# The last 64 tokens of an image as a whole chunk of 128 on TensorE, with new step costs for the planner

## The chip, the core and the metric

The kernel runs on one NeuronCore of a Trainium2 chip. The metric is the device time of one execution in microseconds (us), lower is better. The kernel before was run three times: 1931.54, 1933.95 and 1940.33 us; the median is 1933.95 us.

## What is computed

The input x is 16 images of 56 x 56 positions with 128 channels, float32 throughout. The reference has three parts in a row, each added to its input:

```
x = x + window_attention(group_norm(x))      # 7x7 windows, shifted by 3, 4 heads of 32
t = x as tokens: 16 images of 3136 tokens of 128
t = t + linear_attention(layer_norm(t))      # q, k = elu(.)+1; running sums of k*v over time
t = t + recurrent(layer_norm(t))             # Wx with batch norm; y_t = sigmoid(wx_t + y_{t-1} V^T)
```

Linear attention is computed in chunks: inside a chunk a product of q and k, masked to be causal, and between chunks a running state of 128 x 129 (the sum of k times v, and of k). 3136 tokens are 24 chunks of 128 and one chunk of 64.

## The kernel before, in words

**Stages.** The first stage, up to about 1729 us of the profiled span, treats the images one after the other, overlapped. The second, some 200 us long, is the recurrent scan with its output. The change is in the first stage alone.

**Work of one image in the first stage.** The tokens of an image lie in an SBUF buffer `xt` with 128 tokens on the partitions, in 25 columns of 128 channels, and are handled in seven groups (`GROUPS`, L238): six of four chunks of 128 tokens, and a last one of one chunk of 64 tokens, here called the short group. `chunks_of` (L277) gives a group's part of `xt`; for the short group that is 64 partitions.

- `turned` (L576): each group is transposed on TensorE (`transpose_group`, L558, instruction line L562); ScalarE copies the result to the image buffer `xw` (L604, L606), VectorE takes its statistics (L614). A small chain follows for group normalisation: VectorE L657 to L679, TensorE L661 and L675, GpSimd `again` (L652, L653) and a power (L683), ScalarE L687, TensorE L692.
- `window_row` (L733), eight times an image, one row of eight windows each: VectorE gathers the windows (`gather_windows`, L747), TensorE projects (L757, L784), scores (L808, 64 matmul instructions on weight tiles of 32 x 49), GpSimd subtracts the maximum and scales (L834, L853), TensorE transposes (L863) and mixes (L882, 64 instructions on tiles of 49 x 32), ScalarE writes the result to `oT_buf` (`mix_out`, L917).
- `token_group` (L1031), seven times an image: GpSimd adds the output bias (L1044), TensorE projects (`project`, L1054), VectorE adds (L1063). `layer_scale` (L948) then takes statistics (L958), makes a scale on GpSimd (`join`, L965 to L972), scales (L978) and transposes (L562). TensorE makes q and k (L1095, twice), v (`values`, L1142), transposes k (L1165, not in the short group), the products of k and q (`products`, L1180), the outputs (`attend`, L1209 and L1212) and the state (`gather`, L1220, not in the short group). A second `layer_scale` and a product (L1309) prepare the recurrent part; ScalarE stages it (L1329), and SyncE's DMA queue stores it (L1351) and the tokens (L1015).

One float32 matmul is two instructions in the trace; a transpose is one. The weight tile of an instruction is given as rows*columns. In the short group L562 works on weights of 64*128, L1054, L1142, L1180 and L1209 on 128*64, and L1212 on 64*64; L1095 and L1309 have 128*128 weights as everywhere, and 64 columns to stream.

**What sets the order.** Every piece of work is a `Step` with an engine, a cost and a lag (the time until its result is there). A planner, `Plan` (L54), runs a list schedule over the steps with these numbers, thirty passes at most, each ranked by a backward pass over the one before, and keeps the order with the shortest planned span. That order is emitted engine by engine as the program; on the chip each engine takes its steps in that order and waits by semaphores. `part(g, full, mini)` (L566) picks a cost for a full group or for the short one. The steps share three PSUM banks (`b`), two PSUM pairs (`a`) and single or double SBUF buffers.

Two lines of the short group's steps:

```
n = xg.shape[0]                                                   # 128, or 64 in the short group
nc.tensor.transpose(pt[:, n * cc : n * (cc + 1)], xg[:, cc, :], ident[:n, :n])
...
t["oT"][:, t0 + np * cc : t0 + np * (cc + 1)]                     # np is 64 in the short group
```

Of the kernel before, what the change touches and what calls it, by code (L numbers as in the profile page):

```python
# [206 lines left out]
def tile_conv_attn_hybrid(  # L207
# [19 lines left out]
    nc = tc.nc  # L227
# [11 lines left out]
    GROUPS.append((T // GT * GT, [T % GT]))  # L239
    assert 0 < T % GT <= CK  # L240
    NG = len(GROUPS)
# [35 lines left out]
    def chunks_of(g, xt):  # L277

        return xt[: GROUPS[g][1][0], G * g : G * g + len(GROUPS[g][1]), :]

    def tokens_of(g, image):
# [89 lines left out]
    with ExitStack() as s1:  # L371
# [65 lines left out]


        nc.gpsimd.memset(xw_bufs[1], 0.0)
        nc.sync.dma_start(  # L440
# [117 lines left out]
        def transpose_group(pt, xg):  # L558

            n = xg.shape[0]  # L560
            for cc in range(xg.shape[1]):
                nc.tensor.transpose(  # L562
                    pt[:, n * cc : n * (cc + 1)], xg[:, cc, :], ident[:n, :n]
                )
# [11 lines left out]
        def turned(b, t, loaded, xw_buf, rank):  # L576
# [7 lines left out]
            for g in range(NG):  # L584
# [3 lines left out]
                def turn(g=g, bt=bt):  # L588
                    t0, t1 = group_tokens(g)
                    o[g] = bank(bt, P, t1 - t0)  # L590
                    transpose_group(o[g], chunks_of(g, t["xt"]))

# [16 lines left out]
                def stat(g=g):  # L609
                    if o["st"] is None:  # L610
# [8 lines left out]
                    "PE",  # L619
                    part(g, (0.43, 0.60), (0.06, 0.23)),  # L620
                    rk,
# [5 lines left out]
                    "ACT",  # L627
                    part(g, (0.62, 0.75), (0.18, 0.30)),
                    rk,
# [6 lines left out]
                        "DVE",  # L636
                        part(g, (0.62, 0.70), (0.11, 0.19)),
                        rk,
# [94 lines left out]
        def window_row(b, u, i, o, t, taken, normed, xw_buf, oT_buf, rank):  # L733
# [187 lines left out]
            st = plan.step  # L921
            xk = st("DVE", (0.45, 0.53), rank, gather_windows, [*taken, last_value[i % 2]], drops=[xw_buf])
            pq = st("PE", (0.67, 0.83), rank, lambda: proj(0, "pq", bq), [xk, *normed, last_score[i % 2]], takes=[bq])
# [17 lines left out]
            mi = st("PE", (0.85, 0.92), rank, mix, [tu, vo], takes=[apa], drops=[pT, v])  # L941
            cost = (0.82, 0.94) if u < NU - 1 else (1.20, 1.32)
            return st("ACT", cost, rank, mix_out, [mi], takes=[oT_buf], drops=[apa])
# [4 lines left out]
        def layer_scale(t, g, d, key, rank, after, drops=()):  # L948
# [27 lines left out]
            def scale():  # L976
                d["xn"] = own(xn, P, G, C)[:np, :nk]
                nc.gpsimd.tensor_tensor(  # L978
                    d["xn"],
                    xg,  # L980
                    d["rs"].unsqueeze(2).to_broadcast([np, nk, C]),
                    ALU.mult,
                )

            def turn():
                d["pt"] = bank(bt, P, nk * np)
                transpose_group(d["pt"], d["xn"])

            xn, bt = Buf("xn"), Buf("b")
            s = plan.step("DVE", part(g, (0.78, 0.87), (0.20, 0.28)), rank, stats, after)  # L990
            s = plan.step("POOL", part(g, (2.13, 2.17), (1.20, 1.24)), rank, join, [s])
            sc = plan.step(
                "POOL",
                part(g, (1.01, 1.05), (0.30, 0.34)),
                rank,
# [6 lines left out]
                "PE",  # L1002
                part(g, (0.43, 0.60), (0.06, 0.23)),
                rank,
# [26 lines left out]
        def token_group(b, g, i, t, turned_x, rows_done, oT_buf, xt_buf, rank):  # L1031
# [19 lines left out]
            def project():  # L1051
                d["po"] = bank(bo, np, nk, C)
                for cc in range(nk):
                    nc.tensor.matmul(  # L1054
                        d["po"][:, cc, :],
                        t["oT"][:, t0 + np * cc : t0 + np * (cc + 1)],
                        wout_sb,
                        start=True,
                        stop=True,
                    )  # L1060

            def plus_attention():
                nc.vector.tensor_tensor(xg, d["po"], xg, ALU.add)  # L1063

            bo = Buf("b")
            s0 = st("POOL", part(g, (1.23, 1.27), (0.34, 0.38)), rank - SLOT, plus_bias, [turned_x])
            s1 = st(
                "PE",
                part(g, (0.88, 1.04), (0.22, 0.38)),
                rank,  # L1070
# [9 lines left out]
            def x_out():  # L1080
                d["xnT"] = own(xnT, P, GT)[:, :nt]
                nc.scalar.copy(d["xnT"], d["pt"])  # L1082

# [5 lines left out]
            def feature(j):  # L1089
# [3 lines left out]
                def proj():  # L1093
                    d[f"p{j}"] = bank(bp, P, nt)
                    nc.tensor.matmul(  # L1095
                        d[f"p{j}"],
                        awc_sb[:, j * P : (j + 1) * P],
                        d["xnT"],
                        start=True,
                        stop=True,  # L1100
                    )
# [14 lines left out]
                def larger():  # L1116
                    d[key] = own(f, P, GT)[:, :nt]
                    nc.vector.scalar_tensor_tensor(  # L1118
                        d[key],
                        d[f"p{j}"],  # L1120
                        bqk_one[:, j : j + 1],
                        d[f"r{j}"],
                        ALU.add,
                        ALU.max,
                    )

                p = st("PE", part(g, (0.87, 1.03), (0.12, 0.28)), rank, proj, [xo, *first], takes=[bp], drops=[xnT])
                s = st("ACT", part(g, (0.58, 0.68), (0.25, 0.35)), rank, relu, [p], takes=[r])
                s = st("ACT", part(g, (0.53, 0.63), (0.20, 0.30)), rank, expo, [s])
                return st("DVE", part(g, (0.66, 0.75), (0.16, 0.25)), rank, larger, [s], takes=[f], drops=[r, bp]), f  # L1130

# [4 lines left out]
            def chunk(f, cc):  # L1136
                return f[:, np * cc : np * (cc + 1)]

            def values():
                d["pv"] = bank(bv, np, nk, C)  # L1140
                for cc in range(nk):
                    nc.tensor.matmul(  # L1142
                        d["pv"][:, cc, :],
                        chunk(d["xnT"], cc),
                        awc_sb[:, 2 * P : 3 * P],
                        start=True,
                        stop=True,
                    )
# [8 lines left out]

            bv = Buf("b")
            s = st("PE", part(g, (0.88, 1.04), (0.22, 0.38)), rank, values, [xo, *first, *last_pd[i % 2]], takes=[bv], drops=[xnT])
            vo = st("DVE", part(g, (0.60, 0.69), (0.20, 0.28)), rank, v_out, [s], drops=[bv])  # L1160

            def turn_k():
                d["pk"] = bank(bk, np, nk, C)
                for cc in range(nk):
                    nc.tensor.transpose(d["pk"][:, cc, :], chunk(d["f1"], cc), ident)  # L1165

            def k_out():
                d["k"] = own(k, P, G, C)[:np, :nk]
                nc.scalar.copy(d["k"], d["pk"])
# [7 lines left out]
            def products():  # L1177
                d["pA"] = bank(bA, np, nk, np)
                for cc in range(nk):
                    nc.tensor.matmul(  # L1180
                        d["pA"][:, cc, :],
                        chunk(d["f1"], cc),
                        chunk(d["f0"], cc),
                        start=True,
# [3 lines left out]
            def A_out():  # L1188
                d["A"] = own(A, P, G, CK)[:np, :nk, :np]
                nc.vector.tensor_tensor(  # L1190
                    d["A"],
                    d["pA"],
                    causal_sb[:np, :np].unsqueeze(1).to_broadcast([np, nk, np]),
                    ALU.mult,
                )

            s = st("PE", part(g, (0.89, 1.05), (0.11, 0.28)), rank, products, [fq, fk], takes=[bA], drops=[bfk])
            Ao = st("DVE", part(g, (0.60, 0.69), (0.13, 0.22)), rank, A_out, [s], takes=[A], drops=[bA])


            apn = Buf("a")

            def attend(cc):
                c = G * g + cc
                if cc == 0:
                    d["pn"] = pairs[apn.place][:np]
                to = d["pn"][:, cc // 2, (C + 1) * (cc % 2) : (C + 1) * (cc % 2 + 1)]
                if c > 0:
# [3 lines left out]
                nc.tensor.matmul(  # L1212
                    to, d["A"][:, cc, :], v1[:np, cc, :], start=c == 0, stop=True
                )

            def gather(cc):
                c = G * g + cc
                if c == 0:
# [3 lines left out]
                    d["k"][:, cc, :],  # L1222
                    v1[:np, cc, :],
                    start=c == 0,
# [49 lines left out]
            def divisors():  # L1274
                na, ni = max(nk // 2, 1), min(nk, 2)
                pn4 = d["pn"][:, 0:na, 0 : ni * (C + 1)].rearrange(
                    "p a (i c) -> p a i c", i=ni
# [37 lines left out]
            def xs_out():  # L1315
# [17 lines left out]
            s = st("ACT", part(g, (0.47, 0.58), (0.11, 0.22)), rank, xf_out, [s], takes=[xfT], drops=[bt])  # L1333
            s = st("PE", part(g, (0.87, 1.03), (0.12, 0.28)), rank, whole, [s], takes=[bw], drops=[xfT])
            bs = st("DVE", part(g, (0.62, 0.70), (0.11, 0.19)), rank, batch_stats, [s], drops=[bw])
            bss.append(bs)

            xs = st(
                "ACT",
                part(g, (0.66, 0.77), (0.12, 0.22)),  # L1340
                rank,
# [429 lines left out]
```

## Time and profile before

| | |
|---|---|
| median of three runs | 1933.95 us |
| the profiled execution, its time | 1933.64 us |
| its span, first to last instruction | 1931.8 us |
| mean granted TensorE clock over the span | 0.983 |
| first projection (L757) starts | 24.2 us |
| second stage starts (L1521) | 1728.9 us |
| DMA, whole span | 160.98 MB, mean 83 GB/s |

The profile gives for each engine the time it was busy and the number of its instructions. The end of a matmul is modelled and overlaps the next one's start, so the time that a TensorE step takes from the stream is read from the distance between its start and the next one's, here called spacing. A group's row has the line, the engine, the operation, what it writes and reads, the weight tile, the shapes and the count; then busy us and the mean in ns of one instruction, and the idle time of the engine ahead of them with what ended it.

### The profile page before, as it was taken

The page shows a single profiled execution, that of the slowest core. Times are in us where ns is not written, and L with a number is a line of the kernel's source. Part 1 is how long each engine was busy: PE and PEld are TensorE (multiplying, and loading weights), DVE is VectorE, ACT ScalarE, POOL GpSimd, SP SyncE. Part 2 cuts the span into 40 slices and gives each one's busy share as a digit, 9 for nine tenths or more (in the row PEclk, how much of TensorE's full clock was granted, in tenths as well). Part 3 has the DMA queues.
Part 4 walks back from the last instruction along what each step waited for, and adds up shares of the span by engine and source line. Part 5 has one row for each costly group of instructions (what it writes and reads, how often), then busy time and mean ns, then how long its engine had stood idle before and what let it go on. Part 6 is the DMA issues. An engine that isn't in the chain of part 4 may idle for free.

```text
span 1931.8 us, 65226 instructions
## 1 busy us (share of the span) xinstructions
PE 1846.2 (96%) x27070; PEld 1489.0 (77%) x27070; DVE 1401.3 (73%) x3227; ACT 1306.1 (68%) x3235; POOL 1159.8 (60%) x2025
## 2 busy tenths in 40 slices
PE   6999999999999999999999999999999999989787
PEld 4878777886887778877878787787878777857666
DVE  5777677777677777776777777767777767757678
ACT  4776766767666777667767676766777766647455
POOL 5766767566667667576767576676757756640000
PEclk8999999999999999999999999999999999989889
DMA  4112121111111121211111111212111020555998
GB/s 134 30 30 70 35 62 36 31 63 41 58 45 48 34 70 30 63 46 59 35 36 58 40 61 33 64 34 65 40 35 42 19 85 19 179 202 191 410 408 291
DMA packets 150462, 160.98 MB, mean 83 GB/s; under 512 B 5456, under 2 KB 134224, under 8 KB 148368
## 3 DMA queue, kind: packets, MB, share of 16 engines
q1 hardware_dynamic: 148576, 155.96, 23.8%
q8 instruction: 215, 3.52, 0.8%
q10 hardware_dynamic: 1584, 0.79, 0.1%
q14 instruction: 87, 0.71, 0.1%
HBM read 80.34 MB, written 76.38 MB: 81 GB/s over the span
## 4 chain that ended last, share of the span: by engine, by line
PE 77%; DVE 8%; ACT 5%; DMA 4%; issue 2%; POOL 2%; SPq 0%; ACTq 0%; DVEq 0%; POOLq 0%
PE bank L757 8%; PE bank L1095 8%; PE bank L784 6%; PE bank L562 6%; PE pair L808 5%; PE pair L863 5%; PE state_bank L1220 5%; PE bank L1054 5%; PE bank L1180 5%; PE pair L1209 4%; PE bank L1142 4%; PE pair L1212 4%; PE pair L882 4%; PE bank L1309 4%; DMA out_dram<-o_a 4%
## 5 line engine op out<-in xcount | busy, mean ns | idle before, releaser
L853 POOL TENSOR_TENSOR p_buf<-p_buf,rc 128x784 f32<-128x784 f32 x128 | 195.1, 1525 | 125.4 <-DVE rc L850 69.5
L834 POOL TENSOR_TENSOR s<-s,mx 128x784 f32<-128x784 f32 x128 | 193.6, 1512 | 102.9 <-DVE mx L831 98.3
L1095 PE MATMUL bank<-xnT,awc_sb 128*128 128x512 f32 (+1 forms) x448 | 210.9, 554 | 2.6 <-ACT xnT L1082 0.9
L1105 ACT ACTIVATE r<-bank,bqk_neg 128x512 f32<-128x512 f32 (+1 forms) x224 | 143.6, 641 | 89.3 <-PE bank L1095 69.8
L1118 DVE SCALAR_TENSOR_TENSOR f<-bank,bqk_one,r 128x512 f32<-128x512 f32 (+1 forms) x224 | 149.9, 669 | 44.3 <-ACT r L1114 36.8
L917 ACT ACTIVATE oT_buf<-pair,gbias 128x28 f32<-128x28 f32 (+4 forms) x576 | 144.1, 354 | 30.6 <-PE pair L882 30.1
L819 DVE TENSOR_TENSOR s<-pair,wmask_sb 128x784 f32<-128x784 f32 x128 | 123.3, 963 | 53.1 <-PE pair L808 41.5
L1209 PEld LDWEIGHTS pair<-state,f 128*128 128x128 f32 (+1 forms) x768 | 121.9, 188 | 48.9 <-issue 29.3
L1220 PE MATMUL state_bank<-v_buf,k 128*128 128x129 f32 x768 | 156.4, 285 | 2.1 <-ACT state L1232 1.7
L1220 PEld LDWEIGHTS state_bank<-v_buf,k 128*128 128x128 f32 x768 | 122.4, 190 | 44.2 <-issue 22.2
L1212 PE MATMUL pair<-v_buf,A 128*128 128x129 f32 (+1 forms) x800 | 155.9, 276 | 0.1
L1209 PE MATMUL pair<-state,f 128*128 128x129 f32 (+1 forms) x768 | 153.5, 281 | 0.3 <-ACT state L1232 0.2
L873 ACT COPY pT<-pair 128x904 f32<-128x904 f32 x128 | 118.5, 926 | 47.5 <-PE pair L863 42.5
L1232 ACT COPY state<-state_bank 128x129 f32<-128x129 f32 x384 | 107.4, 280 | 58.8 <-PE state_bank L1220 54.6
L1044 POOL TENSOR_TENSOR xt_buf<-xt_buf,bout_sb 128x512 f32<-128x512 f32 (+1 forms) x112 | 128.3, 1159 | 30.0 <-PE bank L562 25.9
L1568 ACT ACTIVATE y_a<-z_buf,bsh 128x224 f32<-128x224 f32 x224 | 100.1, 447 | 67.8 <-PE z_buf L1565 66.9
L848 DVE TENSOR_REDUCE sm<-p_buf 128x16 f32<-128x784 f32 x128 | 122.9, 960 | 26.6 <-ACT p_buf L844 25.8
L562 PE MATMUL bank<-ident,xn 128*128 128x128 f32 (+1 forms) x800 | 125.3, 275 | 11.4 <-POOL xn L978 4.0
L1114 ACT ACTIVATE r<-r 128x512 f32<-128x512 f32 (+1 forms) x224 | 130.8, 584 | 3.0
L808 PEld LDWEIGHTS pair<-kT,q_buf 32*49 32x49 f32 x8192 | 105.9, 121 | 30.6 <-issue 18.5
L1565 PE MATMUL z_buf<-y_a,fvT_sb 128*128 128x224 f32 x444 | 127.3, 370 | 0.2 <-ACT y_a L1568 0.2
L831 DVE TENSOR_REDUCE mx<-s 128x16 f32<-128x784 f32 x128 | 122.6, 958 | 1.5
(155 smaller groups left out, 5064.3 us busy)
## 6 DMA issues: line engine op xcount, KB each, us to landing
x_d<-xt_buf SPq DMA_DIRECT2D x96, 256.0 KB, 2.2
xt_buf<-in_x_dram SPq DMA_DIRECT2D x93, 256.0 KB, 2.8
xs_d<-staged SPq DMA_DIRECT2D x15, 1568.0 KB, 6.4
out_dram<-o_a SPq DMA_DIRECT2D x13, 1792.0 KB, 15.3
xw_buf<-x_d SPq DMA_DIRECT2D x8, 2048.0 KB, 22.6
spare<-xs_d SPq DMA_DIRECT2D x4, 1680.0 KB, 17.4
oT_buf<-x_d SPq DMA_DIRECT2D x3, 2048.0 KB, 24.2
xs_ring<-xs_d SPq DMA_DIRECT2D x3, 1680.0 KB, 13.0
```

Of the source, the lines that this page charges most:

```text
L562: nc.tensor.transpose(pt[:, n * cc : n * (cc + 1)], xg[:, cc, :], ident[:n, :n])
L757: nc.tensor.matmul(d[key], o["ws"][:, j * P : (j + 1) * P], xk, start=True, stop=True)
L808: nc.tensor.matmul(sc[64 * hh : 64 * hh + WT, hp, w * WT : (w + 1) * WT], qT[r : r + HD, w * WT : (w + 1) * WT], d["kT"][r : r + HD, w * W ...
L834: nc.gpsimd.tensor_tensor(d["sf"], d["sf"], d["mx"].unsqueeze(2).to_broadcast([P, nb, WT]), ALU.subtract,)
L853: nc.gpsimd.tensor_tensor(prf, prf, d["rc"].unsqueeze(2).to_broadcast([P, nb, WT]), ALU.mult)
L917: nc.scalar.activation(to, piece, AF.Identity, bias=o["bias"][:, 2:3])
L1095: nc.tensor.matmul(d[f"p{j}"], awc_sb[:, j * P : (j + 1) * P], d["xnT"], start=True, stop=True,)
L1105: nc.scalar.activation(d[f"r{j}"], d[f"p{j}"], AF.Relu, bias=bqk_neg[:, j : j + 1], scale=-1.0,)
L1118: nc.vector.scalar_tensor_tensor(d[key], d[f"p{j}"], bqk_one[:, j : j + 1], d[f"r{j}"], ALU.add, ALU.max,)
L1209: nc.tensor.matmul(to, chunk(d["f0"], cc), t["states"][c], start=True, stop=False)
L1212: nc.tensor.matmul(to, d["A"][:, cc, :], v1[:np, cc, :], start=c == 0, stop=True)
L1220: nc.tensor.matmul(t["pd"], d["k"][:, cc, :], v1[:np, cc, :], start=c == 0, stop=True, skip_group_check=True,)
```

## The change

The short group keeps its 64 tokens in DMA, on VectorE's and GpSimd's loads of tokens, and in what is stored. Its TensorE steps work on a whole chunk: transposes read all 128 partitions of the chunk and write 128 columns, and weights have 128 rows and 128 columns. What is behind the 64 tokens comes out in PSUM and is not read, or meets a zero: the causal mask is zero for rows 64 to 127 of the product, so `attend` may take all 128 rows of it. Four memsets on GpSimd at the start set what would otherwise be unset: columns 3136 to 3263 of `oT_buf0`, and partitions 64 to 127 of the last chunk of each of the three `xt` buffers. VectorE's masking of the product (L1190) works on 128 partitions of 64 elements instead of 64. The step costs in the plan are replaced by other numbers. The planner makes a new order from them on all engines; the numbers of instructions by line stay, but for the four memsets.

```diff
+    def whole_chunks(g, xt):
+        return xt[:, G * g : G * g + len(GROUPS[g][1]), :]
...
+        nc.gpsimd.memset(flat(oT_buf0)[:, T : T + CK], 0.0)
+        for xt in xt_bufs:
+            nc.gpsimd.memset(xt[64:, G * (NG - 1), :], 0.0)
...
-            n = xg.shape[0]
             for cc in range(xg.shape[1]):
                 nc.tensor.transpose(
-                    pt[:, n * cc : n * (cc + 1)], xg[:, cc, :], ident[:n, :n]
+                    pt[:, CK * cc : CK * (cc + 1)], xg[:, cc, :], ident
                 )
...
-                    part(g, (0.43, 0.60), (0.06, 0.23)),
+                    part(g, (0.44, 0.60), (0.11, 0.28)),
...
-                    part(g, (0.62, 0.75), (0.18, 0.30)),
+                    part(g, (0.58, 0.71), (0.15, 0.28)),
...
-            xk = st("DVE", (0.45, 0.53), rank, gather_windows, [*taken, last_value[i % 2]], drops=[xw_buf])
+            xk = st("DVE", (0.27, 0.37), rank, gather_windows, [*taken, last_value[i % 2]], drops=[xw_buf])
...
-            cost = (0.82, 0.94) if u < NU - 1 else (1.20, 1.32)
+            cost = (0.91, 1.04) if u < NU - 1 else (1.47, 1.65)
...
-            s = plan.step("POOL", part(g, (2.13, 2.17), (1.20, 1.24)), rank, join, [s])
+            s = plan.step("POOL", part(g, (2.13, 2.17), (1.61, 1.64)), rank, join, [s])
...
-                        d["po"][:, cc, :],
-                        t["oT"][:, t0 + np * cc : t0 + np * (cc + 1)],
+                        po[:, cc, :],
+                        t["oT"][:, t0 + CK * cc : t0 + CK * (cc + 1)],
                         wout_sb,
...
-                p = st("PE", part(g, (0.87, 1.03), (0.12, 0.28)), rank, proj, [xo, *first], takes=[bp], drops=[xnT])
+                p = st("PE", part(g, (0.86, 1.02), (0.17, 0.33)), rank, proj, [xo, *first], takes=[bp], drops=[xnT])
...
             def chunk(f, cc):
-                return f[:, np * cc : np * (cc + 1)]
+                return f[:, CK * cc : CK * (cc + 1)]
...
                         chunk(d["f1"], cc),
-                        chunk(d["f0"], cc),
+                        chunk(d["f0"], cc)[:, :np],
...
-                d["A"] = own(A, P, G, CK)[:np, :nk, :np]
+                d["A"] = own(A, P, G, CK)[:, :nk]
                 nc.vector.tensor_tensor(
-                    d["A"],
+                    d["A"][:, :, :np],
                     d["pA"],
-                    causal_sb[:np, :np].unsqueeze(1).to_broadcast([np, nk, np]),
+                    causal_sb[:, :np].unsqueeze(1).to_broadcast([P, nk, np]),
...
-            s = st("PE", part(g, (0.89, 1.05), (0.11, 0.28)), rank, products, [fq, fk], takes=[bA], drops=[bfk])
+            s = st("PE", part(g, (0.89, 1.05), (0.13, 0.29)), rank, products, [fq, fk], takes=[bA], drops=[bfk])
...
                 nc.tensor.matmul(
-                    to, d["A"][:, cc, :], v1[:np, cc, :], start=c == 0, stop=True
+                    to, d["A"][:, cc, :], v1[:, cc, :], start=c == 0, stop=True
                 )
```

The remaining cost edits are of the same kind and smaller: by at most 0.06 us on the cost of a short group's step and 0.02 us on that of a full group's, and by at most 0.08 us on a lag (`xs_out`).

## The prediction, made before the changed kernel was run

> **What bounds the kernel now.** I read the page first, then the busy time by stage, then TensorE's groups with shapes kept apart, then TensorE's timeline around a short group, and VectorE's gathers last.
>
> ```profile
> span 1931.8 us, 65226 instructions
> PE 1846.2 (96%) x27070; PEld 1489.0 (77%) x27070; DVE 1401.3 (73%) x3227; ACT 1306.1 (68%) x3235; POOL 1159.8 (60%) x2025
> PE 77%; DVE 8%; ACT 5%; DMA 4%; issue 2%; POOL 2%; SPq 0%; ACTq 0%; DVEq 0%; POOLq 0%
> ```
>
> TensorE is busy 96% of the span and carries 77% of the chain that ended last. By stage (us, then each engine's busy us and instructions, clock, DMA share, GB/s):
>
> ```profile
> 24.20:1728.90 1704.70, 1668.96 (x26065) 1343.65 (x26063) 1241.74 (x2953) 1185.49 (x2957) 1139.20 (x1983) 1.00 0.17 52
> 1728.90:1931.80 202.90, 168.45 (x970) 138.21 (x970) 150.68 (x254) 114.46 (x258) 5.34 (x15) 0.91 0.84 326
> ```
>
> In the first stage TensorE has the full clock, and VectorE at 73%, ScalarE at 70% and GpSimd at 67% all have room; DMA is at 0.17. So a nanosecond less in TensorE's stream is, to first order, a nanosecond less in the stage. The scan after it is untouched.
>
> The groups of the short chunk, beside their whole brothers:
>
> ```profile
> L1054 PE MATMUL bank<-wout_sb,oT_buf 128*128 128x128 f32 x768 | 103.3, 277 | 1.1 <-DVE gst L614 0.6 <-ACT v L796 0.4
> L562 PE MATMUL bank<-ident,xn 64*128 64x64 f32 x32 | 8.7, 273 | 3.8 <-DVE v_buf L1151 3.0 <-ACT xfT L1305 0.8
> L1054 PE MATMUL bank<-wout_sb,oT_buf 128*64 128x128 f32 x32 | 6.9, 298 | 0.0
> L1142 PE MATMUL bank<-awc_sb,xnT 128*64 128x128 f32 x32 | 6.9, 298 | 0.0
> ```
>
> These durations are latencies of pipelined work: 298 against 277 ns would make the whole change worth almost nothing. What counts is the spacing of starts, from the timeline (start us, modelled us, name):
>
> ```profile
> 781.06 1.02 PE L1095 MATMUL bank<-xnT,awc_sb 128*128 128x512 f32 x2
> 782.01 0.27 PE L562 MATMUL bank<-ident,xn 64*128 64x64 f32 x1
> 782.22 0.49 PE L1220 MATMUL state_bank<-v_buf,k 128*128 128x129 f32 x2
> ...
> 798.32 1.02 PE L1095 MATMUL bank<-xnT,awc_sb 128*128 128x512 f32 x2
> 799.18 1.05 PE L1054 MATMUL bank<-wout_sb,oT_buf 128*128 128x128 f32 x8
> 800.07 1.06 PE L784 MATMUL bank<-ws,oT_buf 128*128 128x128 f32 x8
> 801.06 0.43 PE L1209 MATMUL pair<-state,f 128*64 128x129 f32 x2
> 801.42 0.43 PE L1212 MATMUL pair<-v_buf,A 64*64 64x129 f32 x2
> 801.78 1.12 PE L1095 MATMUL bank<-xnT,awc_sb 128*128 128x512 f32 x2
> ```
>
> The same L1095 step takes 0.86 us ahead of a 128*128 step (798.32 to 799.18) and 0.95 ahead of a 64*128 one (781.06 to 782.01). Eight whole matmul instructions of L784 take 0.99 ahead of the 128*64 step; L1054's eight take 0.89, so 0.22 a pair. The short pairs L1209 and L1212 take 0.36 each. A step on part of the array costs on going in and on coming out.
>
> **The change part by part.**
>
> *TensorE's steps.* I took the median spacing of each step, where nothing is waited for, over the whole trace. Short, and then the whole-chunk spacing: L562 202 ns, a quarter of 437 for four: 109, three times an image; L1054 363 and 893/4 = 223; L1142 362 and 223; L1209 364 and 224; L1212 361 and 223; L1180 258. For the last no whole row is there with 64 streamed columns and a mask to follow; nearest is L1095's short step, also 128*128 with 64 columns, at 170; the bounds are 141 (L661, one column) and 223, and I take 170. Per image: short 606 + 363 + 362 + 364 + 361 + 258 = 2314 ns, whole 327 + 223 + 223 + 224 + 223 + 170 = 1390. Saved 924 ns, times 16 images: 14.8 us.
>
> *Going in.* A whole step before a step on a part takes 92 to 94 ns more (L1212: 317 against 223; L562: 530 against 437; L757: 755 against 663; L784: 987 against 893). In the order before, 98 short steps follow a whole one; a further 30 follow another partial step and pay nothing. That is 98 x 94 = 9.2 us saved. Window steps (L808, L882) also pay on entry: 225 times before, 242 in the changed order, since short steps no longer prepare the array for them: 17 x 94 = 1.6 us lost. Sum on TensorE: 14.8 + 9.2 - 1.6 = 22.4 us.
>
> *A rule against it.* The Trainium skill's page "TensorE: Matmul & The Clock Gate", section "LDWEIGHTS (loading the stationary operand)", has the load grow with the columns, whatever the rows. The rows agree: a weight load of 128*64 is 134 ns, of 128*128 192. Padding L1054, L1142, L1209, L1212 and L1180 then adds ten loads of 58 ns an image, 9.3 us in all, if loads stood on the path; the saving would be 13. "TensorEngine Tiling (Array Packing)", section "Performance Considerations", goes further and wants dimensions up to 64 on smaller tiles. But two whole loads of 192 ns fit under a spacing of 223 ns, so they overlap the stream, while the smaller loads stand under 362. That page's "Key Properties" also says that a switch of tiling mode drains the array. The spacing decides: 22.4.
>
> *Other engines.* L1190 on 128 partitions of 64 instead of 64: row 206 ns before; VectorE's other 128x64 row out of PSUM with two tensors is 272 (L1118). Bounds 0 and 66 ns x 16 = 1 us of VectorE, which has 27% free; I take 0 on the path; if VectorE bound, 1 us. The four memsets: 128x128 rows are 204 ns, so 0.8 us at most on GpSimd. They stand before L439's memset, which ends at 6.2; GpSimd then waits until 10.3 for a DMA, a cover of 4.1 us, so 0; without cover 0.8 once. Work in ScalarE, GpSimd and the DMA queues is the same by instruction; the short transposes write 64 more PSUM columns which nobody reads.
>
> *Order at the start.* VectorE's wait for the mask (L477, 0.96 us, spacing 0.88) now stands before L679 instead of after it, and one gather (0.28) after it instead of before. L679 leads over L683 and L687 to L692, where TensorE waits 8.0 us: +0.6 us, in full.
>
> *Order elsewhere.* The new costs reorder everything: only about a third of TensorE's rows keep their sequence. Waits may move either way. Laid against the spacings above, TensorE loses 101 us to waits between 25 and 1729 us, at 479 places, 343 of all being hits of about 102 ns where a result comes just in time. I expect about as many after. For fewer: the short steps' own costs come near their spacings (0.06 to 0.11 for a transposition), and likewise `mix_out` (0.91 against a spacing of 0.91 for its four ScalarE writes). For more: a faster TensorE outruns the others. Bounds: 10 us less, a tenth, and 14 us more, most of what is freed. I take 0.
>
> *SyncE's queue.* Stores and loads are the same; near the end one store of `xt` precedes the fetches of the scan differently by one place. The first stage's DMA is at 0.17, so 0; the scan's waits for DMA may shift by some 4 us either way (TensorE waits 22.5 us in it for VectorE's sums, which wait for DMA).
>
> *Sum.* 1933.6 (the profiled execution, 0.3 under the median) - 22.4 + 0.6 = 1911.8, so 1912.
>
> **Rivals.**
>
> *Freed time turns into waits.* ScalarE's copies of the state, or GpSimd's chain, end last and TensorE idles. For it: 479 waits already. Against: all others have 27% or more free, and orders overlap two images. With half of 22.4 given back: 1923. Chance 0.2.
>
> *The gathers come too late: slower.* The new plan prices `gather_windows` at 0.27 us instead of 0.45.
>
> ```profile
> L747 DVE COPY x_buf<-xw_buf x64: 301/368/4827, 18.8 to 1638.3; 128x392 f32<-128x392 f32 x64
> L747 DVE COPY oT_buf<-xw_buf x64: 301/368/1816, 19.1 to 1646.4; 128x392 f32<-128x392 f32 x64
> ```
>
> The columns are min/median/max ns. The median is 368, but 40 of the 128 take over 700 ns, together 41 us beyond 300 each; each of these lasts while GpSimd runs its large operations and ends soon after one ends. Behind a gather on VectorE's queue stand L819, L831, L614 and the sums for the attention; L757 on TensorE waits for it, and everything on TensorE behind that. TensorE loses 13 us ahead of L757 now. If the tighter price exposes all of these gathers, 41 - 13 = 28 us are added: 1912 + 28 = 1940. It decides from 22 us of newly exposed time on. Against: bank and window buffers, not the price, often set when a gather may start, and steps in between cover it. Chance 0.05.
>
> *The parts do not cost what the spacing says.* If only going in is saved and a whole chunk needs as long as the short one: 1933.6 - 7.6 + 0.6 = 1927. Against: L1209's whole pair is at 224 ns in 368 places. Chance 0.05.
>
> **How the numbers follow.** Main case 0.7, at 1912. Its own range, with waits -10 to +10 and the scan +-4: 1900 to 1924. Half given back 0.2, the gathers 0.05, the parts 0.05. The range 1899 to 1926 leaves out the gathers, the parts and the ends of the main case. A measurement of this kernel can tell about 0.5% from no change: below 1924.3 is faster, above 1943.6 slower. Faster: nearly all of the main case and 0.17 of the second, 0.86; within: 0.10; slower: 0.04, from the far end of the gathers and from a bad order.
>
> **What would show it right or wrong.** The 64*128, 128*64 and 64*64 groups vanish; L1054, L1142, L1209 and L1212 have spacings of 223 ns in the short group too; the scan starts (L1521) at about 1707 instead of 1728.9, while its own length stays at 203. Waits on TensorE between 25 us and L1521 stay near 101 us. It is wrong if L757 waits for L747 by 20 us more, if TensorE's busy share falls well below 96%, or if the scan grows by more than 4 us.

## The result and the profile after

The changed kernel took 1921.27 us in the median of five runs (1920.71 to 1931.54), the kernel before 1934.30 us in the median of five (1931.54 to 1940.33): a ratio of 0.9937, 95% interval 0.991 to 0.9965, some 12 us faster. 1912 was forecast, 22 us faster.

The profiled execution of the changed kernel took 1931.54 us, the longest of its five. Its page says where that comes from only when it is read by stage. First the page's head:

```profile
span 1929.6 us, 65214 instructions
PE 1828.7 (95%) x27070; PEld 1489.8 (77%) x27070; DVE 1405.6 (73%) x3227; ACT 1312.9 (68%) x3235; POOL 1163.0 (60%) x2029
PE 77%; DVE 9%; ACT 5%; DMA 4%; POOL 3%; issue 2%; SPq 0%; ACTq 0%; DVEq 0%; POOLq 0%
```

TensorE's busy time is down 17.5 us with the same number of instructions, the span by 2.2. Then the busy time by stage, from the first projection to the scan's start and from there to the end:

```profile
22.90:1718.70 1695.80, 1649.03 (x26063) 1343.09 (x26063) 1244.56 (x2951) 1191.54 (x2957) 1142.33 (x1983) 0.99 0.17 53
1718.70:1929.60 210.90, 170.23 (x970) 139.25 (x970) 151.07 (x254) 115.11 (x258) 5.37 (x15) 0.90 0.82 314
```

The first stage ends 10.2 us earlier than before (1718.7 against 1728.9), not 21.8. The scan, whose work is the same, took 8.0 us longer in this one execution (210.9 against 202.9). I therefore compare first stages, and take the whole time from the medians.

The groups of the short chunk are gone into the whole ones (800 where there were 768 and 32), and L1195, which was L1180, has its 64 columns on full weights:

```profile
L1224 PE MATMUL pair<-state,f 128*128 128x129 f32 x768 | 151.4, 279 | 0.0
L572 PE MATMUL bank<-ident,xn 128*128 128x128 f32 x800 | 126.3, 277 | 14.0 <-POOL xn L990 5.2 <-DVE v_buf L1166 1.7 <-DVE f L1132 1.6
L1068 PE MATMUL bank<-wout_sb,oT_buf 128*128 128x128 f32 x800 | 109.5, 277 | 2.1 <-ACT kT L784 1.1 <-ACT v L808 0.5 <-ACT staged L1344 0.3
L1195 PE MATMUL bank<-f,f 128*128 128x64 f32 x32 | 5.7, 260 | 0.0
```

TensorE's timeline around a short step of L1068 (which was L1054):

```profile
1677.28 0.39 PE L1224 MATMUL pair<-state,f 128*128 128x129 f32 x2
1677.50 0.39 PE L1227 MATMUL pair<-v_buf,A 128*128 128x129 f32 x2
1677.72 0.39 PE L1068 MATMUL bank<-wout_sb,oT_buf 128*128 128x128 f32 x2
1677.94 0.39 PE L1235 MATMUL state_bank<-v_buf,k 128*128 128x129 f32 x2
```

The step before it takes 0.22 and it takes 0.22 itself: neither going in nor coming out costs anything. The median spacings of the short steps over the trace are 223 ns (L1068, L1157), 170 (L1195) and 109 to 111 (L572).

What eats the rest are waits. These are the ones that VectorE ends in the first stage, after 25 us, with a longest over 0.9 us, from the waits of the changed kernel (us in total, times, longest):

```profile
PE bank L1324 <- DVE f L1132: 2.5, 1, 2.5
PE bank L1109 <- DVE xt_buf L1077: 2.3, 1, 2.3
PE bank L796 <- DVE v_buf L1166: 1.3, 1, 1.3
PE bank L1180 <- DVE v_buf L1166: 1.1, 1, 1.1
PE bank L1180 <- DVE f L1132: 1.0, 1, 1.0
```

Before, the longest such wait in the first stage was 3.0 us (L562 for L1151), and all the others 0.9 or less. The profile's waits leave out gaps under 150 ns and what the modelled ends of matmuls cover. So I use two numbers for each kernel, both from the starts in TensorE's timeline, as in the prediction: **work** is the sum of the median spacings of all steps of the first stage in their order, with 94 ns for each entry to a partial step; **waits** is by how much the real distances exceed them after the first 25 us, whatever made them longer. Before: work 1606.5 us, waits 101.0. After: 1584.2 and 114.4. Of the 13.4 us more, VectorE ends 11.5 as far as the trace names who ended a wait (31.0 against 19.5, in the table below).

### The profile page after: what moved, and what is told of

Read it like the earlier page. It is cut to its first block, busy times and chain, and to the rows that moved or that the text cites. A ratio compares the mean times of both kernels' runs of the same rounds, so it can differ in the third digit from the quotient of the medians.

```text
span 1929.6 us, 65214 instructions
## 1 busy us (share of the span) xinstructions
PE 1828.7 (95%) x27070; PEld 1489.8 (77%) x27070; DVE 1405.6 (73%) x3227; ACT 1312.9 (68%) x3235; POOL 1163.0 (60%) x2029
## 4 chain that ended last, share of the span: by engine, by line
PE 77%; DVE 9%; ACT 5%; DMA 4%; POOL 3%; issue 2%; SPq 0%; ACTq 0%; DVEq 0%; POOLq 0%
PE bank L1109 8%; PE bank L769 8%; PE bank L572 6%; PE bank L796 5%; PE pair L820 5%; PE pair L875 5%; PE bank L1195 4%; PE pair L894 4%; PE bank L1157 4%; PE state_bank L1235 4%; PE pair L1224 4%; PE pair L1227 4%; PE bank L1068 4%; PE bank L1324 4%; DMA out_dram<-o_a 3%
## 5 line engine op out<-in xcount | busy, mean ns | idle before, releaser
L1109 PE MATMUL bank<-xnT,awc_sb 128*128 128x512 f32 (+1 forms) x448 | 212.0, 556 | 3.5 <-DVE xt_buf L1077 2.3
L1132 DVE SCALAR_TENSOR_TENSOR f<-bank,bqk_one,r 128x512 f32<-128x512 f32 (+1 forms) x224 | 149.4, 667 | 44.0 <-ACT r L1128 36.4
L1227 PE MATMUL pair<-v_buf,A 128*128 128x129 f32 x800 | 155.1, 275 | 0.1
L1224 PEld LDWEIGHTS pair<-state,f 128*128 128x128 f32 x768 | 123.6, 191 | 40.4 <-issue 26.8
L1224 PE MATMUL pair<-state,f 128*128 128x129 f32 x768 | 151.4, 279 | 0.0
L1583 ACT ACTIVATE y_a<-z_buf,bsh 128x224 f32<-128x224 f32 x224 | 100.7, 450 | 74.5 <-PE z_buf L1580 47.0
L572 PE MATMUL bank<-ident,xn 128*128 128x128 f32 x800 | 126.3, 277 | 14.0 <-POOL xn L990 5.2
L1344 ACT COPY staged<-bank 128x448 f32<-128x448 f32 (+7 forms) x288 | 83.6, 383 | 67.0 <-PE bank L1324 33.2
## 6 DMA issues: line engine op xcount, KB each, us to landing
oT_buf<-x_d SPq DMA_DIRECT2D x3, 2048.0 KB, 24.2
```

The costliest lines, as they stand in the source:

```text
L572: nc.tensor.transpose(pt[:, CK * cc : CK * (cc + 1)], xg[:, cc, :], ident)
L1109: nc.tensor.matmul(d[f"p{j}"], awc_sb[:, j * P : (j + 1) * P], d["xnT"][:, :nt], start=True, stop=True,)
L1132: nc.vector.scalar_tensor_tensor(d[key][:, :nt], d[f"p{j}"], bqk_one[:, j : j + 1], d[f"r{j}"], ALU.add, ALU.max,)
L1224: nc.tensor.matmul(to, chunk(d["f0"], cc), t["states"][c], start=True, stop=False)
L1227: nc.tensor.matmul(to, d["A"][:, cc, :], v1[:, cc, :], start=c == 0, stop=True)
```

## The experiments

Costs and shapes can be taken apart, because the order depends on the planner's numbers and not on the shapes: by line, every engine of shapes_only has the order of the kernel before, and every engine of costs_only that of the changed kernel, but for the four memsets. Each ratio is to runs of the kernel before made alongside; their medians in the three groups of experiments were 1934.5, 1934.3 and 1932.0 us.

| kernel | work us | waits us | of these ended by VectorE | scan starts us | median us | ratio (95%) |
|---|---|---|---|---|---|---|
| before | 1606.5 | 101.0 | 19.5 | 1728.9 | 1934.3 | 1 |
| changed | 1584.2 | 114.4 | 31.0 | 1718.7 | 1921.3 | 0.9937 (0.991 to 0.9965) |
| shapes_only | 1584.1 | 102.5 | 22.5 | 1708.2 | 1916.7 | 0.9913 (0.9893 to 0.9932) |
| costs_only | 1607.0 | 107.2 | 26.5 | 1734.2 | 1940.3 | 1.0026 (1.0017 to 1.0035) |
| gather_old_price | 1583.5 | 112.4 | 34.9 | 1717.7 | 1920.4 | 0.992 (0.9904 to 0.9936) |
| gather_mean_price | 1583.9 | 98.5 | 17.4 | 1703.8 | 1909.2 | 0.9875 (0.9855 to 0.9895) |
| margin_lo | 1583.6 | 113.2 | 31.5 | 1716.9 | 1924.4 | 0.9955 (0.9938 to 0.9972) |
| margin_hi | 1584.1 | 118.2 | 31.2 | 1722.5 | 1930.4 | 0.9986 (0.9975 to 0.9998) |
| gather_080 | 1584.1 | 95.2 | 22.5 | 1699.5 | 1907.8 | 0.9868 (0.9844 to 0.9893) |
| shapes_gather_mean | 1583.7 | 103.2 | 25.6 | 1708.3 | 1912.5 | 0.9895 (0.9878 to 0.9911) |
| g080_margin_lo | 1584.6 | 111.2 | 25.7 | 1716.6 | 1921.4 | 0.9943 (0.9927 to 0.996) |
| g080_margin_hi | 1584.3 | 100.7 | 21.5 | 1705.2 | 1909.6 | 0.9878 (0.9861 to 0.9894) |
| shapes_margin_lo | 1584.1 | 115.1 | 18.6 | 1720.9 | 1924.6 | 0.9952 (0.9936 to 0.9969) |
| shapes_margin_hi | 1583.7 | 101.3 | 18.3 | 1706.7 | 1915.0 | 0.9905 (0.9889 to 0.9922) |

Work, waits and starts are from one profiled execution of each, the medians from four or more runs. The share of VectorE counts steps over 60 ns late whose releaser the trace names; for more than a third of the waits none is named.

**Shapes alone.** All 19 cost lines are as before, such as:

```diff
-            xk = st("DVE", (0.27, 0.37), rank, gather_windows, [*taken, last_value[i % 2]], drops=[xw_buf])
+            xk = st("DVE", (0.45, 0.53), rank, gather_windows, [*taken, last_value[i % 2]], drops=[xw_buf])
```

> The change's TensorE shapes with all the old step costs. Its instructions stand in exactly the order of the kernel before on every engine (but for the four memsets). TensorE's own work falls by some 22 us as in the changed kernel. Theory A, the new order brings the added waits (TensorE's waits after 25 us were 101 us before and 114 us after the change): waits stay at about 101 us, the scan starts near 1707 us, the time is about 1912 us (-22). Theory B, a faster TensorE outruns the other engines in any order: waits rise to about 114 us, the scan starts near 1719 us, the time is about 1921 us (-13), as the changed kernel.

Work fell by 22.4 us and waits rose by 1.5; the scan starts 20.7 us earlier. Its first stage (work of engines as above):

```profile
24.20:1708.20 1684.00, 1645.62 (x26064) 1344.51 (x26062) 1243.37 (x2953) 1183.22 (x2956) 1139.33 (x1983) 1.00 0.17 53
```

The stage is 20.7 us shorter than before, and only TensorE's busy time is clearly less. So theory A holds and B falls: in the old order a faster TensorE hardly waits more. By time the old order is the faster one, 1916.7 us against the changed kernel's 1921.3, but the intervals of the two ratios overlap (0.9893 to 0.9932 and 0.991 to 0.9965). The median lies 18 us below the one before (the ratio says 17), 5 us over what was expected; the run-to-run range of 10 us does not let me say where those are.

**Costs alone.** This is the kernel before with the 19 cost lines of the change and no other edit.

> The change's step costs with the old shapes: the order of the changed kernel on every engine, the short group on parts of the array as before. TensorE's own work stays at about 1606 us. Theory A (the order brings the waits): waits of about 112 to 114 us instead of 101, the time about 1946 us (+12), slower than before. Theory B (outrunning): nothing is faster, so waits stay near 101 us and the time near 1934 us.

Nothing on TensorE got faster and the time rose by 0.26%, about 5 us, as did the start of the scan (1734.2):

```profile
22.90:1734.20 1711.30, 1669.59 (x26063) 1340.81 (x26063) 1241.19 (x2951) 1191.08 (x2957) 1144.62 (x1983) 1.00 0.17 52
```

The order is worse by itself. By A the waits should have been 112 to 114 and the time 1946; they were 107.2 and 1940.3, halfway to B. The two halves alone add 1.5 and 6.2 us of waits, both together 13.4, so that some 6 us arise only where the new order meets the faster TensorE, or are the spread of single executions. By times the halves do add up: 0.9913 x 1.0026 = 0.9939 against 0.9937 measured.

**One price put back, and one raised.** The edits of the changed kernel:

```diff
-            xk = st("DVE", (0.27, 0.37), rank, gather_windows, [*taken, last_value[i % 2]], drops=[xw_buf])
+            xk = st("DVE", (0.45, 0.53), rank, gather_windows, [*taken, last_value[i % 2]], drops=[xw_buf])   # gather_old_price
+            xk = st("DVE", (0.65, 0.73), rank, gather_windows, [*taken, last_value[i % 2]], drops=[xw_buf])   # gather_mean_price
```

> The changed kernel with one cost put back: gather_windows at (0.45, 0.53) instead of (0.27, 0.37). Theory C, the low price of the gathers makes the waits: waits back to about 101 us, time about 1911 us. Theory A in its plain form (any new order draws its waits anew, whichever price is behind it): somewhere within 1911 to 1931 us, with waits between 100 and 120 us. Theory B: 1921 us.

> The changed kernel with gather_windows priced near its mean, (0.65, 0.73), instead of near its median, (0.27, 0.37); the row of L747 in the profile before has means of 627 and 732 ns against a median of 368. Theory C: better still than the old price, 1905 to 1911 us, with waits under 101 us. Theory A: anywhere within 1911 to 1931 us. Theory B: 1921 us.

The old price changed nothing that can be told: 112.4 us of waits. So the lower price of the gathers was not what made the change's order bad, and theory C falls in that form. The price near the mean took 16 us of waits away and 12 us of time: as C had it, and 2 us under the range of A. That is either what an honest price of the gathers brings, or another draw.

**Is it the draw?** A margin that the planner adds to every lag but those of TensorE's and SyncE's steps is moved by 4%. It changes no cost, and all those lags alike, by 5 ns:

```diff
-    MARGIN = 0.12
+    MARGIN = 0.115       # margin_lo, and on other kernels g080_margin_lo, shapes_margin_lo
+    MARGIN = 0.125       # margin_hi, g080_margin_hi, shapes_margin_hi
```

> The changed kernel with nothing altered but the planner's safety margin on every lag, 0.115 instead of 0.12 us: no step is priced better or worse than another, yet the order is a new one. Theory A in its plain form (each order draws its waits anew, by some 10 us either way): TensorE's waits after 25 us anywhere within 95 to 120 us, time 1905 to 1930 us, and not the same as with 0.125. Theory D (the low price of the gathers makes bad orders, and a price near their mean makes good ones): waits stay near 114 us and the time near 1921 us.

> As the run before with 0.125 instead of 0.12 us. Theory A: again anywhere within 95 to 120 us of waits, 1905 to 1930 us, apart from its neighbour by several us. Theory D: near 114 us and 1921 us, as its neighbour.

Waits of 113.2 and 118.2 us beside 114.4, and 1924 and 1930 us beside 1921. Both theories allowed the first; the second is 9 us off for D. An edit that singles out no step moves this kernel by 9 us.

**A price over the mean, and the price near the mean with the other old costs.** As above, with (0.80, 0.88) in the changed kernel, and with (0.65, 0.73) in shapes_only.

> The changed kernel with gather_windows priced over its mean, (0.80, 0.88). With (0.27, 0.37), (0.45, 0.53) and (0.65, 0.73) TensorE's waits after 25 us were 114, 112 and 98 us. Theory D: about as good as the price near the mean, waits 95 to 101 us, time 1905 to 1912 us. Theory A: anywhere within 95 to 120 us, 1905 to 1930 us.

> The change's shapes with the old costs, and gather_windows alone priced near its mean, (0.65, 0.73). Theory D: waits fall from the 102.5 us of the same kernel with (0.45, 0.53) by as much as in the changed kernel, to some 90 us, time 1903 to 1906 us. Theory A: waits within 95 to 120 us, time 1905 to 1930 us.

gather_080 is the fastest of all, 1907.8 us, 1.3% under the kernel before and beyond the interval of the changed kernel. Its first stage:

```profile
24.20:1699.50 1675.30, 1640.63 (x26061) 1339.44 (x26059) 1239.99 (x2952) 1182.45 (x2957) 1143.99 (x1982) 1.00 0.17 53
```

But with the other old costs the same step in price brought nothing in waits (103.2 against 102.5), against D. Three margins for each family of costs follow.

> The changed kernel with gather_windows at (0.80, 0.88), and the planner's margin 0.115 instead of 0.12 us, which makes another order. With the gathers at (0.27, 0.37) three margins gave waits of 113, 114 and 118 us on TensorE after 25 us, and 1921 to 1930 us; with (0.80, 0.88) and 0.12 it was 95 us and 1908 us. Theory D (a gather price at or over its mean makes good orders): waits 93 to 101 us, time 1904 to 1914 us. Theory A (the low value of one order was luck): waits 95 to 120 us, time 1908 to 1930 us, most likely over 1914 us.

> As the run before, with a margin of 0.125 us. Theory D: waits 93 to 101 us, time 1904 to 1914 us. Theory A: waits 95 to 120 us, time 1908 to 1930 us, most likely over 1914 us.

> The change's shapes with all the old costs, and a margin of 0.115 instead of 0.12 us. With 0.12 it had waits of 102.5 us and 1916.7 us. If the old costs make better orders than the new ones as a family: waits 98 to 107 us, time 1908 to 1918 us. If the order of before was just one good draw: waits 105 to 120 us, time 1917 to 1930 us.

> As the run before, with a margin of 0.125 us. Old costs better as a family: waits 98 to 107 us, time 1908 to 1918 us. One good draw: waits 105 to 120 us, time 1917 to 1930 us.

Within each family of costs the three orders spread: new costs 113, 114, 118; old costs 101, 102.5, 115; new costs with the gathers at 0.80: 95, 101, 111. With D alone g080_margin_lo should have stayed under 101, and it had 111; with old costs better as a family, shapes_margin_lo should have stayed under 107, and it had 115. Their neighbours g080_margin_hi and shapes_margin_hi did come out as D and the family had it. So what holds is theory A in its plain form: each order draws its waits, with a spread of 5 to 16 us of the same prices. Its ranges were wide, so that little could have spoken against it; what speaks for it is that the times go with the waits. The intervals of the ratios lie apart for changed and margin_hi, for gather_080 and g080_margin_lo, and for shapes_only and shapes_margin_lo, so that these are no differences of single executions.

What can be said for D is narrower. The waits that VectorE ends were 31 to 35 us in the four orders that have the new costs with a gather price of 0.27 or 0.45, on the new shapes, and 17 to 26 us in all other kernels on the new shapes. There the prices leave a mark. Which of the other 18 edits makes it was not tried. Nor do bad draws always go through VectorE: shapes_margin_lo waits 115.1 us, of which VectorE ends 18.6.

**How a gather makes TensorE wait.** VectorE's timeline in the changed kernel, around one of the first stage's two longest waits for VectorE:

```profile
584.10 3.79 DVE L759 COPY oT_buf<-xw_buf 128x392 f32<-128x392 f32 x1 [0.92 <-PE bank L796]
587.81 0.96 DVE L831 TENSOR_TENSOR s<-pair,wmask_sb 128x784 f32<-128x784 f32 x1
588.80 0.97 DVE L843 TENSOR_REDUCE mx<-s 128x16 f32<-128x784 f32 x1
589.69 0.96 DVE L860 TENSOR_REDUCE sm<-p_buf 128x16 f32<-128x784 f32 x1
590.68 0.25 DVE L862 RECIPROCAL rc<-sm 128x16 f32<-128x16 f32 x1
590.85 0.63 DVE L1077 TENSOR_TENSOR xt_buf<-bank,xt_buf 128x512 f32<-128x512 f32 x1
```

And TensorE's at the end of the wait:

```profile
588.51 0.74 PE L572 MATMUL bank<-ident,xn 128*128 128x128 f32 x4
591.53 2.02 PE L1109 MATMUL bank<-xnT,awc_sb 128*128 128x512 f32 x2 [2.29 <-DVE xt_buf L1077]
593.35 1.87 PE L1324 MATMUL bank<-xfT,fwTc_sb 128*128 128x512 f32 x2
```

The gather (L759, which was L747) lasts 3.79 us where its median is 0.37; four operations of VectorE stand behind it, and then the one whose bank L1109 needs. The projection that reads the gather does not wait. The other long wait, 2.5 us of L1324, ends at 271.0 us, behind a gather of 4.77 us and L1132, which stands behind the gather:

```profile
265.40 4.77 DVE L759 COPY x_buf<-xw_buf 128x392 f32<-128x392 f32 x1
...
270.97 2.04 PE L1324 MATMUL bank<-xfT,fwTc_sb 128*128 128x512 f32 x2 [2.48 <-DVE f L1132]
```

costs_only, in the same order, has both waits too, of 2.2 and 1.8 us. But the kernel before has one of the kind as well, and shapes_only has the same one:

```profile
477.53 4.83 DVE L747 COPY x_buf<-xw_buf 128x392 f32<-128x392 f32 x1
482.28 0.68 DVE L1151 TENSOR_TENSOR v_buf<-bank,bv_sb 128x512 f32<-128x512 f32 x1
...
483.11 0.34 PE L562 MATMUL bank<-ident,xn 64*128 64x64 f32 x1 [2.96 <-DVE v_buf L1151]
```

So the chain explains 4.8 us of the changed order's waits and 3.0 of the old one's, 1.8 of the 13.4 us between them. The rest is spread. Of TensorE's idle gaps between 25 us and the scan, those over 0.9 us went from 6 of together 11.5 us to 10 of 17.0, and those of 0.15 to 0.9 us from 53 of 20.9 us to 65 of 26.3.

A long wait also costs more than its own length, because the clock granted to TensorE stood at half around the end of each of these three (0.50, ahead of the DMA share, in this line by stage):

```profile
591.60:595.00 3.40, 3.40 (x4) 1.27 (x5) 1.44 (x5) 0.66 (x1) 3.15 (x8) 0.50 0.00 0
```

In that stretch L1109 and L1324 take 1.82 and 1.70 us from start to start, where the median of both is 0.86. From 270.8 us the clock was 0.50 for 3.4 us too, and in the kernel before from 482.0 to 488.8 us. The steps in these stretches ran 1.8, 1.7 and 2.9 us over their medians, and this stands in the number called waits. From 30 us to the scan it is, counted in the same way, 4.8 us in the changed kernel, 3.7 before, and 0.7 to 6.7 in the fourteen kernels. So it is 1 of the 13.4 us, and the "full clock" of the prediction was full but for a few microseconds. Not every long wait was followed by it: in gather_080 one of 2.2 us at 378.0 us was not.

## Why the prediction was right or wrong, point by point

**TensorE's own work: right.** -22.4 us forecast, -22.3 found in the changed order and -22.4 in the old one. That is also the point where the weight-load rule of the Trainium skill and the spacing parted (section "LDWEIGHTS (loading the stationary operand)" of "TensorE: Matmul & The Clock Gate"): by the rule with the loads on the path the saving would have been 13. These sums count the changed kernel as the prediction did; the check that does not is shapes_only, whose first stage is 20.7 us shorter. The 94 ns for an entry held too; entries fell from 323 to 242.

**The guess of 170 ns for L1180: right.** It is 170.

**Waits: wrong, and it is the term that was mis-sized.** The step said "I take 0", with bounds of -10 and +14; it was +13.4, near the upper bound and beyond the +10 that the main case's own range was built with. The reason given for more waits, that a faster TensorE outruns the others, is not enough: shapes_only shows 1.5 us for that in the old order. The order drew 6.2 us by itself, as costs_only shows. The last 6 us appear only with both together; whether they are the faster TensorE in the new order or the spread of single executions stays open, since by the medians the order costs about 5 us with either shapes. What I read as a reason for fewer waits, costs that come near the spacings, did not bring fewer. That the time still lies inside 1899 to 1926 was in part luck: with the margin at 0.125 the same change takes 1930.4 us.

**The rivals.** The rival of half given back forecast 1923 and came nearest, but not by its mechanism: it had TensorE outrun ScalarE and GpSimd, and the old order shows hardly any outrunning, while in the new one VectorE ends 11.5 of the 13.4 us, as far as they are named. The gathers did not come too late at L757 (steps over 60 ns late there wait some 11 us against 12), and nothing like 28 us was added. Their long durations do reach TensorE, by the queue behind them. That the spacing does not tell the costs is refuted by shapes_only.

**The start: wrong in sign, small.** +0.6 us was forecast; the first projection started 1.3 us earlier (22.9 against 24.2). TensorE's timeline before, and in the changed kernel:

```profile
22.80 1.63 PE L492 MATMUL bank<-awT_sb,mean_sb 128*128 128x384 f32 x2
...
13.42 1.63 PE L503 MATMUL bank<-awT_sb,mean_sb 128*128 128x384 f32 x2
...
21.62 1.44 PE L704 MATMUL bank<-gm,ws 128*128 128x1 f32 x6 [6.14 <-ACT ws L699]
22.92 1.65 PE L769 MATMUL bank<-x_buf,ws 128*128 128x392 f32 x2
```

L503 (which was L492), which stood right ahead of the projections and took 1.42 us there, now lies in the wait for L699. The step looked at VectorE's order alone; what TensorE could do in the wait was left out. Nor did the +0.6 us arrive: L691 (which was L679) started 0.73 us later, but the power behind it on GpSimd took 0.62 us where it had taken 1.22 while VectorE's mask L477 ran, and L704 started only 0.13 us later (21.62 against 21.49).

**The scan: beyond its bound of 4 us in the profiled execution.** It took 8.0 us longer, and TensorE's waits for VectorE's sums in it were 28.2 us against 22.5. The median execution was 10.3 us shorter than this one; how much of that is the scan is not recorded. Over the fourteen profiled executions the scan took 200.5 to 211.4 us; in the three over 210 us TensorE waited 33 to 35 us in it, in the others 26 to 32. Whether the order of the last stores or the DMA's own variation makes it long was not tried.

**The four memsets and L1190: no trace of a cost.** shapes_only has them, and its first stage is 20.7 us shorter where work and waits make it 20.9.

The balance of the first stage: -22.3 (work) + 13.4 (waits after 25 us) - 1.4 (waits before) = -10.3, against -10.2 measured.

## What to carry to other kernels

Read the cost of a small matmul step from the distances between starts, to its neighbours on both sides, and not from its duration: 298 against 277 ns hid 363 against 223, and 94 ns more in the step before. When a change also gives a scheduler other costs, split it into shapes and costs before judging either, and try a few neutral edits of the planner: here an edit of 4% to a margin moved the time by up to 14 us, as much as the change itself. Before blaming one kind of event for the difference, look for it in the kernel before as well. A schedule in which one kind of step has a median of 0.37 us and a mean of 0.68 can be tried with the mean or more as its price; it gave the best version here, 1907.8 us, but not in every order.

## What the runs showed of the hardware that was not expected

A copy on VectorE from SBUF to SBUF (L747, 128x392) takes 0.30 us at least and up to 4.83. All 40 that take over 0.7 us lie beside GpSimd's operations, and 39 of them end some 0.2 us after one of these ends. VectorE's addition out of PSUM with more elements (L1063, 128x512) stays between 0.63 and 0.69 us in all 96. The Trainium skill has a rule for it ("SBUF — State Buffer", section "Who interferes with whom"): a VectorE operation in a mode that uses both ports and a GpSimd operation exclude each other, and the second to issue waits for the whole instruction of the first. The trace agrees with the exclusion beside GpSimd's large operations, and in 36 of the 40 one such operation ended while the gather lasted. It does not show it beside the small ones: 19 gathers of 0.30 to 0.41 us lie wholly inside one of GpSimd's operations on 128x4. Whether a gather is in such a mode no run here shows. And a wait can go beyond one instruction: in the changed kernel the gather of 4.77 us at 265.4 us stood through five GpSimd operations that followed each other without a gap, the first of them nearly over at its start, and ended before the sixth did.

Entering a partial weight tile costs the step before it 92 to 94 ns, be it a transpose (L562), a pair (L1212) or a projection (L757, L784), and a pair of matmuls on 128*64 holds TensorE for 362 ns where one on 128*128 holds it for 223.
